# Neighbours' weights in a PSUM bank, key monomials spread over three chunks, and layer 2's first loads ahead of the fall-back loops

## The chip, the cores and the metric

The kernel runs on one core of a Trainium2 chip. The metric is device time in microseconds, from the start to the end of one execution. The kernel before took 4456.89 us (median of 3 runs, 4449.6 to 4462.39). The execution that was profiled took 4452.14 us, and its profile spans 4450.3 us. The mean TensorE clock granted in it was 0.842 of full speed.

Engine names: PE is TensorE (PEld its weight loads), DVE is VectorE, ACT is ScalarE, POOL is GpSimd, and SP issues most of the DMAs. SBUF is the large on-chip memory, PSUM the smaller one into which PE writes, in eight banks. L840 is line 840 of the kernel.

## The reference, cut to what matters

Four graph layers work on 2708 nodes with 128 channels and a dense 2708 x 2708 matrix `adj`, about 0.15% of which (with the diagonal) is not zero. Each layer is x = x + layer(relu(layernorm(x))). The change lies in layer 1 and at the start of layer 2:

```python
# layer 1: attention, 128 heads d of 8 channels, over all nodes
q = (x @ Wq.T).reshape(d, n, h)          # k and v in the same way
a = jnp.einsum('dnh,dmh->dnm', q, k) * scale
a = a + spatial_encoding + edge_encoding # both are adj
a = jax.nn.softmax(a, axis=2)
out = jnp.einsum('dnm,dmh->dnh', a, v)
return out.reshape(n, h * d) @ Wo.T

# layer 2: mean over the graph, two weights, batch norm
deg = adjacency_matrix.sum(axis=1, keepdims=True)
agg = adjacency_matrix.T @ node_features / deg
h = agg @ W_n.T + b_n + node_features @ W_c.T + b_c
# then normalised over the nodes, scaled, relu
```

## The kernel before, in words

The nodes lie in 22 row tiles of up to 128 rows, the last of 20. Layer 0 and the projections to q, k and v come first; layer 1's heads run from about 468 to 3923 us of the span; layers 2 and 3 follow.

**The heads.** Layer 1 never forms the 2708 x 2708 logits. It expands the exponential into monomials of the eight channels of q and of k. For each head d:

- `keys(d)` has GpSimd multiply the key monomials `bk` and `fk` together: twelve multiplications, given out one at a time by the generator `features` (with `mul_g`, whose multiplications are recorded at L1010). `with_values(d, h)` then has GpSimd form `y`, the monomials times the values, for each half h of the row tiles (also L1010).
- `queries(d)` does the same for q on DVE (L1007), reading one operand in PSUM (`q_ps`).
- `moments` has PE sum `fk` times `y` over the nodes in `m_ps` (L1048), and `weighted` has DVE multiply that by constants (L1058).
- For each of six chunks of up to four row tiles (`NCH` is 6), `turn` has PE transpose query monomials into `f_ps` (L1074), which ACT copies to `fT` (L1076); `evaluate` has PE multiply them with the moments into `g_ps` (L1086), and DVE multiply the result by `bq` (`z`, L1094) and sum it (`o_raw`, L1100).

**The neighbours.** Where `adj` isn't zero, a correction is added for each true neighbour. `from_neighbours` does this in 121 blocks, each of one neighbour for each row of a tile. Per block, GpSimd gathers `c_kv` (and once per tile `c_q`) with an indirect DMA; `logits` has DVE multiply keys with queries (`c_z`, L840) and reduce that to `c_c`, one number per row and head (L844); `weigh` has ACT take the exponential in place (L852) and scale it by the edge's weight (L854); `values` of the block before has ACT copy `c_c` into the ninth column (L869), DVE multiply values with `c_c` (L870) into `c_v`, or for a tile's first neighbour straight into `c_acc`, and GpSimd add `c_v` to `c_acc` (L879). A finished tile is stored to `more_n` by an indirect DMA (L887).

**What sets the order.** Everything in the heads is inside `with tc.manual_schedule()`, so each engine takes its instructions in the order in which the program text issues them. Waits between engines are put in from the tiles that they share. In each chunk the loop runs `evaluate`, three steps of `queries`, the next `turn`, a part of `moments`, and then on average `PACE` = 1.45 steps of the generator `first`. This generator runs a search for the neighbours, a re-ordering of q, k and v by node, the sorting of rows, and then `from_neighbours`, which occupies about 1320 to 3322 us. All twelve multiplications of `keys(d + 2)` are issued in one go in chunk 0; `with_values` follows in chunks 2 and 5.

**After the neighbours.** When `first` is done, the list `beside` is worked on, three calls of `step` per chunk. It has 32 times `normalise(g)` (DMAs bring the sums and the corrections of four heads, GpSimd adds them at L930, DVE divides at L932 and L933, SP stores `o_c`) and 22 times `project_out` (SP loads `o_cr`, L499; PE multiplies it with `woT` in four groups of two, L505, each into a buffer of `ps_t`; DVE adds each group to `x_sb`, L508). What remains when the heads end is drained in the loop `while beside or under_way`.

**Between layers 1 and 2.** L1186 to L1223 check from bounds whether the expansion is accurate enough and the neighbour lists long enough. The result, `flag`, is the trip count of three fall-back loops, which in this case run zero times. At a loop's entry each engine waits for all the others and for all DMA queues. Then layer 2 opens its pools, loads and transposes its weights (`wnT`, `wcT`), normalises x (`norm_relu`), spreads the reciprocal degrees over all partitions (`diB`, 22 pairs of a small matmul and an ACT copy), and multiplies `adj`, loaded by row tiles into four buffers (L1339), into `pg` (L1341).

`ps_t`, with two buffers of one bank each, serves `f_ps`, the groups of `project_out` and some transposes. With `m_ps` (1), `g_ps` (2 buffers of two banks) and `q_ps` (1) all eight banks are in use.

Of the kernel before, what the change touches and what calls it, by code (L numbers as in the profile page):

```python
# [9 lines left out]
FP = mybir.dt.float32  # L10
AF = mybir.ActivationFunctionType
# [38 lines left out]
def gnn4_kernel(  # L50
# [75 lines left out]
    few = keep.tile([P, 1], FP, name="few")  # L126

# [388 lines left out]
    with ExitStack() as ph:  # L516
# [8 lines left out]
        ps_t = ph.enter_context(tc.tile_pool(name="l1_pst", bufs=2, space=PSUM))  # L525
        ps_m = ph.enter_context(tc.tile_pool(name="l1_psm", bufs=1, space=PSUM))
        ps_g = ph.enter_context(tc.tile_pool(name="l1_psg", bufs=2, space=PSUM))
        ps_q = ph.enter_context(tc.tile_pool(name="l1_psq", bufs=1, space=PSUM))

# [272 lines left out]
        def from_neighbours():  # L802
# [6 lines left out]
            qs, kvs, cs, accs = {}, {}, {}, {}  # L809
            done = []  # L810
# [23 lines left out]
            def logits(b):  # L834
                t, s0, w = todo[b]
                sz = rows[t][1]
                cs[b] = sm.tile([P, S, C], FP, name="c_c")
                for e in range(w):
                    z = tm.tile([P, C, HEAD], FP, name="c_z", tag="tmp")
                    nc.vector.tensor_tensor(  # L840
                        z[:sz], kvs[b][:sz, e, :, 0], qs[t][:sz], ALU.mult
                    )
                    yield
                    nc.vector.reduce_sum(cs[b][:sz, e], z[:sz], axis=AX.X)  # L844
                    yield
# [169 lines left out]
        def keys(d):  # L1015

            k = got[d // GRP][0][:, d % GRP, :, k_at]
            fks[d] = fp.tile([P, NT, F_ALL], FP, name="fk")
            run(features(mul_g, k, bks[d % 2], fks[d]))
# [86 lines left out]
        with tc.manual_schedule():  # L1106
# [4 lines left out]
            keys(0)  # L1111
# [3 lines left out]
            keys(1)  # L1115
# [10 lines left out]
            for d in range(D):  # L1126
                asked = queries(d + 1) if d + 1 < D else iter(())
                for c in range(NCH):
                    if d + 2 < D and c == 0:
                        while len(got) <= (d + 2) // GRP:  # L1130
                            run(soon.pop(0))
                        keys(d + 2)
# [29 lines left out]
                if (d + 2) % GRP == 0 and (d + 2) // GRP + 1 < NG:  # L1162
                    soon.append(prepare((d + 2) // GRP + 1, got))
            while beside or under_way:
# [4 lines left out]
    with ExitStack() as ph:  # L1169
        gp = ph.enter_context(tc.tile_pool(name="l1g", bufs=1))  # L1170
        gw = ph.enter_context(tc.tile_pool(name="l1g_w", bufs=2))
        g_l = ph.enter_context(tc.tile_pool(name="l1g_l", bufs=1, space=PSUM))
        g_t = ph.enter_context(tc.tile_pool(name="l1g_t", bufs=1, space=PSUM))
        g_o = ph.enter_context(tc.tile_pool(name="l1g_o", bufs=1, space=PSUM))
        q_f = dram.tile([N, P, HEAD], FP, name="q_f")
        k_f = dram.tile([N, P, HEAD], FP, name="k_f")
        v_f = dram.tile([N, P, VW], FP, name="v_f")
        o_f = dram.tile([N, P, HEAD], FP, name="o_f")

        nc.vector.memset(top, 0.0)
        p2 = gp.tile([C, 2], FP, name="p2")
        for e in range(2):
            pt = g_t.tile([P, BK], FP, name="g_tr", tag="tr")  # L1186
            nc.tensor.transpose(pt[:C, :P], most2[:, e], ident)
            nc.vector.tensor_reduce(p2[:, e : e + 1], pt[:C, :P], axis=AX.X, op=ALU.max)
        nc.vector.tensor_tensor(top[:, 0:1], p2[:, 0:1], p2[:, 1:2], ALU.mult)
        nc.vector.tensor_tensor(top[:, 1:2], p2[:, 0:1], p2[:, 1:2], ALU.max)  # L1190
        nc.vector.tensor_reduce(top[:, 2:3], nval, axis=AX.XY, op=ALU.max)
        nc.vector.tensor_reduce(top[:, 3:4], nval, axis=AX.XY, op=ALU.min)
        low = gp.tile([P, 1], FP, name="low")
        nc.vector.tensor_reduce(low, least, axis=AX.X, op=ALU.min)
        nc.vector.tensor_tensor(top[:, 3:4], top[:, 3:4], low, ALU.min)
        nc.vector.tensor_scalar_mul(top[:, 3:4], top[:, 3:4], -1.0)
        nc.vector.tensor_reduce(low, below, axis=AX.X, op=ALU.max)
        nc.vector.tensor_tensor(top[:, 3:4], top[:, 3:4], low, ALU.max)
        nc.vector.tensor_tensor(top[:, 3:4], top[:, 3:4], full, ALU.max)
        pt = g_t.tile([P, BK], FP, name="g_tr", tag="tr")  # L1200
        nc.tensor.transpose(pt[:4, :P], top, ident)
        t4 = gp.tile([4, 1], FP, name="top4")
        nc.vector.tensor_reduce(t4, pt[:4, :P], axis=AX.X, op=ALU.max)
        pt = g_t.tile([P, BK], FP, name="g_tr", tag="tr")
        nc.tensor.transpose(pt[:1, :4], t4, ident[:4, :4])
        bnd = gp.tile([1, 6], FP, name="bound")
        nc.vector.tensor_copy(bnd[:, :4], pt[:1, :4])
        nc.vector.tensor_scalar(
            bnd[:, 4:5], bnd[:, 0:1], MAX_LOGIT**2, None, ALU.is_le
        )  # L1210
        nc.vector.tensor_scalar(bnd[:, 2:3], bnd[:, 2:3], float(MAX_ADJ), None, ALU.is_le)
        nc.vector.tensor_tensor(bnd[:, 4:5], bnd[:, 4:5], bnd[:, 2:3], ALU.mult)
        nc.vector.tensor_scalar(bnd[:, 1:2], bnd[:, 1:2], MOST**2, None, ALU.is_le)
        nc.vector.tensor_tensor(bnd[:, 4:5], bnd[:, 4:5], bnd[:, 1:2], ALU.mult)
        nc.vector.tensor_scalar(bnd[:, 5:6], bnd[:, 3:4], 0.0, None, ALU.is_le)
        nc.vector.tensor_scalar(ovf, bnd[:, 5:6], -1.0, 1.0, ALU.mult, ALU.add)
        pt = g_t.tile([P, BK], FP, name="g_tr", tag="tr")
        nc.tensor.matmul(pt[:, :1], ones[0:1], bnd[:, 5:6], start=True, stop=True)
        nc.vector.tensor_copy(few, pt[:, :1])
        nc.vector.tensor_tensor(bnd[:, 4:5], bnd[:, 4:5], bnd[:, 5:6], ALU.mult)  # L1220
        flag = gp.tile([1, 2], I32, name="flag")
        nc.vector.tensor_scalar(flag[:, 0:1], bnd[:, 4:5], -1.0, 1.0, ALU.mult, ALU.add)
        nc.vector.tensor_scalar(  # L1223
            flag[:, 1:2], bnd[:, 4:5], -float(C), float(C), ALU.mult, ALU.add
        )
        once = nc.values_load(flag[:, 0:1], min_val=0, max_val=1)
        heads = nc.values_load(flag[:, 1:2], min_val=0, max_val=C)

        with tc.For_i(0, once):
            for r0, sz in rows:  # L1230
                for at, dst in ((0, q_f), (HEAD, k_f), (2 * HEAD, v_f)):
                    b = gw.tile([P, P, dst.shape[2]], FP, name="bounce", tag="b")
                    nc.sync.dma_start(
                        b[:, :sz], qkv_c[:, r0 : r0 + sz, at : at + dst.shape[2]]
                    )
                    nc.sync.dma_start(dst[r0 : r0 + sz].rearrange("r c h -> c r h"), b[:, :sz])

        def flat(src):
            return src.rearrange("r c h -> (r c) h")

        with tc.For_i(0, heads) as d:
            nat = []
            for src in (q_f, k_f, v_f):
                a = gp.tile([P, NT, src.shape[2]], FP, name=f"g_nat{len(nat)}")
                f = flat(src)[bass.ds(d * N, N)]
                load_rows(nc.sync, a, f)
                nat.append(a)
            q, k, v = nat
            kT = gp.tile([HEAD, N], FP, name="g_kT")
            for t, (r0, sz) in enumerate(rows):  # L1250
                pt = g_t.tile([P, BK], FP, name="g_tr", tag="tr")
                nc.tensor.transpose(pt[:HEAD, :sz], k[:sz, t], ident[:sz, :sz])
                nc.vector.tensor_copy(kT[:, r0 : r0 + sz], pt[:HEAD, :sz])
            o = gp.tile([P, NT, HEAD], FP, name="g_o")
            for t, (r0, sz) in enumerate(rows):
                an = gw.tile([P, N], FP, name="g_adj")
                nc.sync.dma_start(an[:sz], adj[r0 : r0 + sz])
                pt = g_t.tile([P, BK], FP, name="g_tr", tag="tr")
                nc.tensor.transpose(pt[:HEAD, :sz], q[:sz, t], ident[:sz, :sz])
                qT = gw.tile([HEAD, P], FP, name="g_qT")  # L1260
                nc.vector.tensor_copy(qT[:, :sz], pt[:HEAD, :sz])
                pl = g_l.tile([P, NC, BK], FP, name="g_l")
                for c, (c0, cw) in enumerate(cols):
                    nc.tensor.matmul(
                        pl[:sz, c, :cw], qT[:, :sz], kT[:, c0 : c0 + cw], start=True, stop=True
                    )
                    nc.vector.scalar_tensor_tensor(
                        an[:sz, c0 : c0 + cw],
                        pl[:sz, c, :cw],
                        0.5,  # L1270
                        an[:sz, c0 : c0 + cw],
                        ALU.mult,
                        ALU.add,
                    )
                mx = gw.tile([P, 1], FP, name="g_mx")
# [326 lines left out]
```

## Time and profile before

| what | value |
|---|---|
| median of 3 runs | 4456.89 us |
| profiled execution | 4452.14 us |
| its span | 4450.3 us |
| PE busy over the span | 3230.9 us, 73% |
| DVE busy | 3549.0 us, 80% |
| ACT busy | 1101.9 us, 25% |
| POOL busy | 2789.4 us, 63% |
| c_z (L840), 121 instructions | 419.5 us, mean 3467 ns |
| c_v (L870), 99 instructions | 244.5 us, mean 2470 ns |

How to read it: busy times count what an engine executes, a stall in the middle of an instruction included. The shares are averages over stages with different limits, so they are not yet a statement on what bounds the kernel. An instruction's line may be that of a helper: all GpSimd multiplications of the heads, whatever they form, are recorded at L1010, and are told apart by their tiles. In the answers shown, `out<-in` are the names of the tiles, `xN` the number of instructions, and `<-DVE x` behind an idle time names what ended it.

### The profile page before, as it was taken

What the parts mean: (1) busy time and instruction counts of PE and PEld (TensorE: products, weight loads), DVE (VectorE), ACT (ScalarE), POOL (GpSimd) and SP (SyncE); (2) the same over time, 40 slices, a digit from 0 to 9 for tenths busy, and PEclk for the clock granted to TensorE, in tenths of its full rate; (3) what the DMA queues carried; (4) which work ended last, traced back from release to release, by engine and by line L of the source; (5) the groups of instructions that cost most, each with busy time, mean ns of one, the idle gap of its engine ahead of it and who ended that gap; (6) DMA issues with size and microseconds to landing.
All of it is one profiled execution on the core that took longest, in us unless ns stands there. A gap on an engine that the chain in (4) does not pass through costs nothing. (4 is left out here: it accounts for less than half of the span.)

```text
span 4450.3 us, 49671 instructions
## 1 busy us (share of the span) xinstructions
PE 3230.9 (73%) x17298; PEld 2879.4 (65%) x17298; DVE 3549.0 (80%) x4852; ACT 1101.9 (25%) x2497; POOL 2789.4 (63%) x2384
## 2 busy tenths in 40 slices
PE   7986788888857777776777766767767788949434
PEld 5953677788756666666666656667657787834223
DVE  5988899987849989999988999999977777840322
ACT  4246233333312222222222222222221111210110
POOL 0001766677767887887878777678876666700266
PEclk9988889899978888888888888888888899979565
DMA  4637344367412222222222222222324454035232
GB/s 181 225 143 304 101 108 123 98 140 178 110 54 80 84 79 90 90 91 81 90 90 91 81 76 96 82 94 97 104 70 105 112 113 96 23 103 203 75 86 70
DMA packets 402006, 480.25 MB, mean 108 GB/s; under 512 B 290672, under 2 KB 322098, under 8 KB 376916
## 3 DMA queue, kind: packets, MB, share of 16 engines
q1 hardware_dynamic: 370140, 308.03, 24.1%
q0 software_dynamic: 31600, 168.86, 11.5%
q8 instruction: 144, 2.36, 0.2%
q14 instruction: 122, 1.00, 0.1%
HBM read 363.13 MB, written 113.67 MB: 107 GB/s over the span
## 5 line engine op out<-in xcount | busy, mean ns | idle before, releaser
L1086 PE MATMUL g_ps<-mw,fT 128*128 128x189 f32 x5632 | 1227.8, 366 | 699.1 <-DVE mw L1058 397.8
L1086 PEld LDWEIGHTS g_ps<-mw,fT 128*128 128x128 f32 x5632 | 1043.2, 215 | 781.0 <-issue 521.9
L1010 POOL TENSOR_TENSOR y<-bk,raw 128x2079 f32<-128x2079 f32 x256 | 976.2, 3814 | 516.1 <-PE m_ps L1048 478.3
L1048 PE MATMUL m_ps<-y,fk 128*128 128x189 f32 (+1 forms) x5632 | 1101.7, 340 | 21.3 <-POOL y L1010 21.3
L1048 PEld LDWEIGHTS m_ps<-y,fk 128*128 128x128 f32 (+1 forms) x5632 | 963.5, 203 | 50.5 <-issue 28.7
L1076 ACT COPY fT<-f_ps 128x512 f32<-128x512 f32 (+1 forms) x768 | 422.7, 550 | 1962.1 <-PE f_ps L1074 1960.1
L1094 DVE TENSOR_TENSOR z<-g_ps,bq 128x756 f32<-128x756 f32 (+1 forms) x768 | 669.4, 872 | 202.4 <-PE g_ps L1086 201.7
L1100 DVE TENSOR_REDUCE o_raw<-z 128x36 f32<-128x756 f32 (+1 forms) x768 | 672.5, 876 | 26.3
L1074 PE MATMUL f_ps<-ident,fq 128*128 128x128 f32 x2816 | 490.3, 299 | 38.9 <-DVE fq L1007 36.2
L1010 POOL TENSOR_TENSOR fk<-bk,raw 128x528 f32<-128x528 f32 (+1 forms) x512 | 508.2, 1021 | 0.0
L1074 PEld LDWEIGHTS f_ps<-ident,fq 128*128 128x128 f32 x2816 | 400.5, 157 | 75.7 <-issue 31.5
L840 DVE TENSOR_TENSOR c_z<-c_kv,c_q 128x1024 f32<-128x1024 f32 (+1 forms) x121 | 419.5, 3467 | 10.6 <-DMA c_kv<-kv_n,srt 10.6
L879 POOL TENSOR_TENSOR c_acc<-c_acc,c_v 128x1152 f32<-128x1152 f32 (+1 forms) x99 | 262.1, 2647 | 165.6 <-DVE c_v L870 119.1
L1010 POOL TENSOR_TENSOR fk<-raw,bk 128x352 f32<-128x352 f32 (+1 forms) x512 | 317.7, 649 | 0.0
L1007 DVE TENSOR_TENSOR fq<-bq,q_ps 128x528 f32<-128x528 f32 (+1 forms) x512 | 288.0, 604 | 0.0
L870 DVE TENSOR_TENSOR c_v<-c_kv,c_c 128x1024 f32<-128x1024 f32 (+1 forms) x99 | 244.5, 2470 | 1.3 <-POOL c_acc L879 1.3
L465 POOL MEMSET qkv<- 128x512 f32 x6 | 6.3, 1083 | 374.8 <-PE l_o L350 255.4
L1010 POOL TENSOR_TENSOR bk<-raw 128x88 f32<-128x88 f32 (+1 forms) x512 | 216.7, 454 | 33.4 <-DMA raw<-qkv_c 32.9
L1420 POOL DMA_INDIRECT g<-gate_d,srt x121 | 122.6, 1013 | 107.7 <-issue 107.7
L825 POOL DMA_INDIRECT c_kv<-kv_n,srt x121 | 137.3, 1135 | 60.2 <-DVE c_acc L870 37.5
L1007 DVE TENSOR_TENSOR fq<-q_ps,bq 128x352 f32<-128x352 f32 (+1 forms) x512 | 171.7, 377 | 0.0
L505 PE MATMUL l_o<-woT,o_cr 128*128 128x128 f32 (+1 forms) x352 | 95.8, 421 | 81.2 <-DMA o_cr<-o_c 40.2
(284 smaller groups left out, 3502.7 us busy)
## 6 DMA issues: line engine op xcount, KB each, us to landing
a_nat<-in_adj_dram SPq DMA_DIRECT2D x32, 1354.0 KB
qkv_c<-qkv SPq DMA_DIRECT2D x5, 6400.0 KB
a<-in_adj_dram SPq DMA_DIRECT2D x21, 1354.0 KB
kv_n<-n_kv SPq DMA_DIRECT2D x32, 672.0 KB
an<-in_adj_dram SPq DMA_DIRECT2D x15, 1354.0 KB
o_g<-o_raw SPq DMA_DIRECT2D x32, 396.0 KB
r_raw<-o_g SPq DMA_DIRECT2D x32, 396.0 KB
r_more<-more_n SPq DMA_DIRECT2D x32, 396.0 KB
```

Source lines behind the costliest of these rows:

```text
L825: nc.gpsimd.indirect_dma_start(out=kvs[b][:sz, e].rearrange("p c e k -> p (c e k)"), out_offset=None, in_=kv_n.rearrange("n c k -> n (c k) ...
L840: nc.vector.tensor_tensor(z[:sz], kvs[b][:sz, e, :, 0], qs[t][:sz], ALU.mult)
L870: nc.vector.tensor_tensor(z[:sz, :, :HEAD], kv[:sz, e, :, 1], c[:sz, e, :, None].to_broadcast([sz, C, HEAD]), ALU.mult,)
L879: nc.gpsimd.tensor_tensor(acc[:sz], acc[:sz], z[:sz], ALU.add)
L1007: nc.vector.tensor_tensor(o, x, y, ALU.mult)
L1010: nc.gpsimd.tensor_tensor(o, x, y, ALU.mult)
L1048: nc.tensor.matmul(pms[d][:, : B_ALL * VW], fks[d][:sz, t], ys[d, h][:sz, m].rearrange("p k b -> p (k b)"), start=t == 0, stop=t == NT - 1,)
L1074: nc.tensor.transpose(pt[:, m], fqs[d][:, t0 + m], ident)
L1076: nc.scalar.copy(fts[d, c][:, :n], pt[:, :n])
L1086: nc.tensor.matmul(pg[:, m, : B_ALL * VW], ft[:, m], mws[d].rearrange("p k b -> p (k b)"), start=True, stop=True,)
L1094: nc.vector.tensor_tensor(z[:, :n], pg[:, :n, : B_ALL * VW].rearrange("p t (k b) -> p t k b", k=VW), bqs[d % 2][:, t0 : t0 + n, None, :B_A ...
L1100: nc.vector.reduce_sum(ros[g][:, t0 : t0 + n, i], z[:, :n], axis=AX.X,)
```

## The change

It has three parts.

1. `c_c` is no longer a tile of the SBUF pool `sm` (two buffers) but one half of a single PSUM tile `c_two`, chosen by the block's parity. `c_two` fills one bank, and for that `ps_t` goes from two buffers to one.
2. `keys` becomes a generator. In `keys(d + 2)` five multiplications are issued in chunk 0, five in chunk 1 and the rest in chunk 2, ahead of `with_values`.
3. The bound check moves ahead of the drain, into the heads' pools; `flag` moves to the pool `keep`. Layer 2's pools are opened before the fall-back loops, and `wnT`, `wcT`, the bias columns, `di`, `diB` and the first four loads of `adj` are issued there; the loops' pools lie on top. `norm_relu` and the adjacency product stay behind the loops.

```diff
-        ps_t = ph.enter_context(tc.tile_pool(name="l1_pst", bufs=2, space=PSUM))
+        ps_t = ph.enter_context(tc.tile_pool(name="l1_pst", bufs=1, space=PSUM))
...
+        ps_c = ph.enter_context(tc.tile_pool(name="l1_psc", bufs=1, space=PSUM))
...
+            c_two = ps_c.tile([P, 2, S, C], FP, name="c_c")
...
-                cs[b] = sm.tile([P, S, C], FP, name="c_c")
+                cs[b] = c_two[:, b % 2]
...
-            run(features(mul_g, k, bks[d % 2], fks[d]))
+            yield from features(mul_g, k, bks[d % 2], fks[d])
...
-                        keys(d + 2)
+                        keyed = keys(d + 2)
+                    if d + 2 < D:
+                        for _ in range(5 if c < 2 else NCH * 3):
+                            next(keyed, None)
...
+            nc.vector.memset(top, 0.0)
+            p2 = sm.tile([C, 2], FP, name="p2")
...
+            nc.vector.tensor_scalar(
+                flag[:, 1:2], bnd[:, 4:5], -float(C), float(C), ALU.mult, ALU.add
+            )
+
             while beside or under_way:
                 if not step(n, NG):
                     n += 1
...
+        with tc.tile_pool(name="l2_ps0", bufs=2, space=PSUM) as ps:
+            wnT = transposed(lp, wk_pool, ps, wn2, "wnT")
+            wcT = transposed(lp, wk_pool, ps, wc2, "wcT")
...
+            diB = lp.tile([P, N], FP, name="diB")
+            for t, (r0, sz) in enumerate(rows):
+                dg = lp.tile([P, P], FP, name="dg", tag="dg", bufs=2)
+                nc.vector.tensor_scalar_mul(dg[:sz, :sz], ident[:sz, :sz], di[:sz, t : t + 1])
+                pd = ps.tile([P, BK], FP, name="d_ps", tag="tr")
+                nc.tensor.matmul(pd[:, :sz], ones[:sz], dg[:sz, :sz], start=True, stop=True)
+                nc.scalar.copy(diB[:, r0 : r0 + sz], pd[:, :sz])
+        for t in range(min(4, NT)):
+            rows_of_adj2(t)
+
+
+        with ExitStack() as gh:
...
+            once = nc.values_load(flag[:, 0:1], min_val=0, max_val=1)
+            heads = nc.values_load(flag[:, 1:2], min_val=0, max_val=C)
```

## The prediction

> **What bounds the kernel now.** I read the windows by stage first, because the 80% that DVE is busy over the whole span mixes stages with different limits. Columns: stretch and us, busy us and (x instructions) of PE, PEld, DVE, ACT, POOL, then the PE clock granted, the DMA share and GB/s.
>
> ```profile
> 468.00:1225.00 757.00, 630.34 (x3693) 590.73 (x3693) 678.27 (x997) 260.86 (x502) 522.04 (x477) 0.91 0.49 120
> 1225.00:3322.00 2097.00, 1468.53 (x7914) 1376.68 (x7913) 1917.43 (x2253) 468.84 (x1182) 1652.94 (x1329) 0.83 0.26 85
> 3322.00:3923.00 601.00, 502.00 (x2847) 473.38 (x2845) 457.11 (x739) 111.89 (x259) 402.30 (x334) 0.91 0.37 85
> 3923.00:3969.00 46.00, 16.33 (x69) 13.94 (x69) 10.60 (x44) 0.00 (x0) 4.74 (x3) 0.58 0.38 96
> 3969.00:4000.00 31.00, 9.77 (x33) 5.44 (x33) 15.96 (x79) 7.28 (x24) 0.13 (x1) 0.57 0.49 189
> ```
>
> The second stretch, where the neighbour blocks run beside the heads, is 47% of the span, and DVE is busy 91% of it (94% in 1445 to 3300, which holds 64 heads of 29.0 us). So DVE sets the pace there. The tile answers say of what its time consists (min/median/max ns):
>
> ```profile
> L840 DVE TENSOR_TENSOR c_z<-c_kv,c_q x121: 1215/3453/14609, 1318.7 to 3300.7; 128x1024 f32<-128x1024 f32 x119, 20x1024 f32<-20x1024 f32 x2
> L870 DVE TENSOR_TENSOR c_v<-c_kv,c_c x99: 1212/1653/8760, 1343.7 to 3322.6; 128x1024 f32<-128x1024 f32 x98, 20x1024 f32<-20x1024 f32 x1
> L844 DVE TENSOR_REDUCE c_c<-c_z x121: 1197/1210/1223, 1322.2 to 3305.5; 128x128 f32<-128x1024 f32 x119, 20x128 f32<-20x1024 f32 x2
> ```
>
> The same 1024 elements take 1.2 us or up to 14.6 us in the first two rows, and always 1.2 us in the reduce. The timeline shows what stands beside a long one (start, duration):
>
> ```profile
> 2078.65 10.53 DVE L840 TENSOR_TENSOR c_z<-c_kv,c_q 128x1024 f32<-128x1024 f32 x1
> ...
> 2076.85 1.39 POOL L1010 TENSOR_TENSOR bk<-raw 128x176 f32<-128x176 f32 x4
> 2078.19 2.38 POOL L1010 TENSOR_TENSOR fk<-raw,bk 128x352 f32<-128x352 f32 x4
> 2080.53 3.85 POOL L1010 TENSOR_TENSOR fk<-bk,raw 128x528 f32<-128x528 f32 x4
> 2084.35 3.75 POOL L1010 TENSOR_TENSOR y<-bk,raw 128x2079 f32<-128x2079 f32 x1
> ```
>
> c_z stands until GpSimd's train of twelve key multiplications and one y is over. Summed over its durations, c_z is 419.5 us busy against 121 x 1.22 = 148, so 271 us are standing; c_v and the first-of-tile c_acc are 292.7 against 147, so 146 (125 of them in 1445 to 3300). By the GpSimd operation running meanwhile, I put c_z's standing in 1445 to 3300 at 147 under y, 82 under keys, 32 under the rest, and c_v's at 62 under keys and 58 under y.
>
> **What the Trainium skill says.** "SBUF — State Buffer", section "Who interferes with whom": a DVE instruction that reads two operands from SBUF shares a port pair with GpSimd under an exclusive lock; with one SBUF operand it doesn't. The trace agrees: z, with g_ps in PSUM, averages 0.87 us over both its forms and never stands, while c_v reaches 8.76. "VectorE: DVE Perf Modes", section "The perf-mode tier table": an fp32 tensor_tensor runs at 1x from SBUF and from PSUM, so moving an operand costs no rate. z's 756 elements in 0.93 us and c_v's unhindered 1024 in 1.21 fit that. "PSUM — Partial Sum Buffer", section "PSUM bank collisions raise a hardware error": two engines must not touch one bank at once, so ACT and DVE have to take turns on it. No trace here shows the price.
>
> **The change part by part**, against the profiled execution's 4452.1 us (span 4450.3 and 1.8 around it), which lies 4.8 under the median 4456.9, inside the three runs' 12.8.
>
> *Weights in PSUM.* c_v and c_acc keep one SBUF operand and lose their 146 us of standing. The 1.21 us stay, and so do c_z's, whose operands are both in SBUF. DVE is 94% busy, so I let 0.9 through: -131.
>
> *Keys over three chunks.* The same twelve multiplications, split as 2.3 us (0.48 + 3 x 0.34 + 0.83) in chunk 0, 3.9 in chunk 1 and 1.7 ahead of y in chunk 2, where 7.8 stood together. An operation that comes at random waits in proportion to the sum of squares of the trains: before 7.8², 3.8², 3.8², after 2.3², 3.9², 5.5², 3.8², so 90 becomes 65, or 0.73. That takes 0.27 of c_z's 261: -70. Heads that come faster (29.0 to some 26.5) put the same GpSimd work into less time: +18 on the 191 left. Net -52, of which I count -45, since the trains may still join where GpSimd is behind. Who waits: y of half 0 is now behind only 1.7 us of keys in its chunk, and `moments` needs the keys only a head later. On GpSimd's queue the gathers and c_acc additions of chunks 1 and 2 now stand behind pieces of keys, those of chunk 0 behind less; DVE waits for them 4.2 us today (c_z for c_kv 2.9, c_v for c_acc 1.3), so this is nothing unless gathers come late. In 468 to 1225, PE and DVE bound without blocks, and in the heads of 3322 to 3923 r_on (59.7 us busy against 28.5 unhindered) gains at most 31 x 0.27 = 8, not counted.
>
> *Turns on the bank.* ACT's copy L869 (0.42 us) now comes after the reduce of the next block, and c_v after that copy, all in one bank. Both fall into one chunk in 0.45 of the blocks (1.45 steps a chunk). Two handovers and the copy are about 0.75 us by these rows: 121 x 0.45 x 0.75 = +40. From 0, if other DVE work lies between, to 121 x 0.75 = +91. ACT's exp and scale (0.31 and 0.40) come after c_v and four steps before they are needed: hidden. Behind a waiting ACT stands fT, for which PE's g_ps waits (73.8 us in 1445 to 3300), so part of ACT's waiting may return there; this is in the upper bound.
>
> *One ps_t buffer for two.* For the transposes it is free: `evaluate` of a chunk already waits for the fT copy that empties the buffer before PE comes to the next `turn`. project_out is not free. With two buffers its first two groups ran in one go, and DVE's additions came later together:
>
> ```profile
> 3600.59 2.02 PE L505 MATMUL l_o<-woT,o_cr 128*128 128x128 f32 x8
> 3604.91 0.67 DVE L508 TENSOR_TENSOR x_sb<-x_sb,l_o 128x128 f32<-128x128 f32 x2
> 3605.25 1.22 PE L505 MATMUL l_o<-woT,o_cr 128*128 128x128 f32 x4 [2.64 <-DVE x_sb L508]
> 3606.50 0.29 DVE L508 TENSOR_TENSOR x_sb<-x_sb,l_o 128x128 f32<-128x128 f32 x1 [0.92 <-PE l_o L505]
> ```
>
> PE's third group already waited 2.64 us. With one buffer each further group in a chunk stands for DVE's addition, and the chunk's turn and `evaluate` with it: some 1.9 us per project (two handovers, at the 0.92 and 0.29 just shown plus a start), 18 projects in the loop: +35, from 10 to 60. In the drain after it the additions follow each other in 0.96 us; eight groups become about 0.6 longer: +5.
>
> *Checks and layer 2 earlier.* The bound check ran from 3964.48 to 3968.74 with nothing beside it; now it stands in the 6.4 us in which PE waited for o_cr: -4.3. diB (22 multiplications and copies) leaves the adjacency product, about 6 us of PE there, but DVE and ACT need the time before: -6 if beside the loads, else +8. The four adjacency loads are 1.354 MB each; they landed at 3989.0 to 3998.4, 19.5 us after SP's first layer-2 load at 3978.87. Now they are issued ahead of the loops, and every engine waits at a loop's entry for all queues. Their buffers lie where the drain's tmp tiles lay, so they start only after the last l_o. On SP nothing else is queued behind them but later layer-2 work. What lay after the empty loops (9.7 us) then lies before them: what is saved behind is paid ahead. norm_relu, which the loads used to cover, then stands alone for part of its 16 us. From -12 to +20; I take +8 with diB in it.
>
> Sum: -131 - 45 + 40 + 35 + 5 - 4 + 8 = -92. Span 4358, and by the median of the runs **4365 us**.
>
> **The rivals.** *GpSimd's standing moves on to c_z (gain of 13 to 40).* After a c_v that no longer stands, c_z meets the train that c_v met before. For it: y causes 147 of c_z's 261 and is unchanged, and GpSimd's own 23.1 us per head is not far under 29. Against: c_v's freedom alone takes 2 us of each head. If half of the 131 comes back, the keys give 20 and the turns cost half: -65 - 20 + 20 + 35 + 5 - 4 + 8 = -21, time 4436.
>
> *Broken trains give more (gain of 150 to 260).* If keys never join y, 0.27 becomes 0.5, and turns hide behind other DVE work: -146 - 112 + 10 + 20 + 5 - 4 + 8 = -219, time 4238. The limit is GpSimd's 23.1 us and c_z's own 2.1 per head, about 25.2, so at most 64 x 3.8 = 243 there.
>
> *Slower: c_v waits for ACT.* ACT works in order and waits 961 us in 1445 to 3300 for f_ps. If L869 stands behind an fT whose transposes PE has not begun, the reduce, the copy and c_v become one chain through PE, and DVE, in order, stands with it. The other terms sum to -132, so it decides at 132/121 = 1.1 us per block; at 1.7 instead of 0.33 it is +206 - 132 = +74: 4531. For it: z waits only 42.7 us for PE today, so PE is little behind. That also speaks against it: PE has finished the turn by the time DVE is at the reduce.
>
> *The change does nothing where it counts.* If both contenders were not ports but memory as a whole, c_v would stand as before. z and the reduce, never long, exclude nearly all of that.
>
> **How the numbers follow.** Forecast (-150 to -40) 0.50; more 0.20; gain of 13 to 40 0.14; within 0.3% (13 us, about what a measurement of this kernel tells from no change) 0.08; slower 0.08. So faster 0.84, same 0.08, slower 0.08. The range leaves out slower, half of same and the far third of the larger gain: 4252 to 4450. The likeliest case alone is 4307 to 4417.
>
> **What would show it.** c_v and c_acc at 1.21 to 1.3 us whatever GpSimd does; c_z's mean from 3.47 to 2.5 to 2.9; heads beside neighbours 26.5 to 27.5 us, DVE still over 90% busy. DVE waits for ACT copy L869 near 40 us in all. PE waits l_o for x_sb above today's 29.4 (in 3330 to 3764), by 20 to 40. No stretch of bound checks before the loops, but adjacency loads ahead of them. I am wrong if DVE's share falls below 85% with heads near 29 us (then a new wait has replaced the standing), if c_z's mean rises, or if the gap from the last l_o to the first pg matmul, 36 us now, passes 56.

## The result, and the profile after

The changed kernel took 4410.15 us (median of 4 runs, 4385.7 to 4422.99) against 4459.64 of the kernel before: ratio 0.9894, 95% interval 0.9853 to 0.9935. A second set of runs gave 4384.33 against 4444.4: 0.9844, 0.9805 to 0.9884. Together that is some 1.3%, about 58 us faster. I had said 92. The direction and the range held; the forecast gain was more than half again as large as what came.

The profiled execution took 4385.7 us (span 4383.9), 66 less than the profiled one of before. Single executions of one kernel lie up to 1.3% apart here. Four of the profiles below are of kernels whose code is the same in the 64 heads that lie wholly beside the neighbours (the changed kernel twice, and the two with `project_out` in one group), and these heads took 1771, 1790, 1777 and 1814 us. A difference between two profiles within that spread is read only together with the timed runs.

The windows of the changed kernel, by the same stages as before (columns as in the prediction):

```profile
465.70:1220.00 754.30, 625.25 (x3701) 584.58 (x3702) 679.26 (x996) 261.49 (x503) 522.84 (x478) 0.93 0.50 121
1220.00:3229.00 2009.00, 1446.03 (x7907) 1354.68 (x7906) 1758.65 (x2250) 452.29 (x1183) 1617.46 (x1330) 0.85 0.27 89
3229.00:3848.00 619.00, 520.56 (x2846) 484.75 (x2844) 438.29 (x741) 111.83 (x258) 402.21 (x334) 0.89 0.36 82
3848.00:3900.00 52.00, 23.03 (x75) 16.08 (x74) 14.32 (x53) 0.27 (x1) 5.20 (x4) 0.52 0.37 88
```

Everything that was won lies in the second stretch: 2097 us became 2009. DVE's busy time there fell by 159 us and its idle time rose by 71 (179.6 to 250.4). The stretch after it became 18 us longer, the drain 6.

The tile answers of the changed kernel say what of DVE's time went:

```profile
L843 DVE TENSOR_TENSOR c_z<-c_kv,c_q x121: 1214/2468/12565, 1305.2 to 3212.7; 128x1024 f32<-128x1024 f32 x119, 20x1024 f32<-20x1024 f32 x2
L873 DVE TENSOR_TENSOR c_v<-c_kv,c_c x99: 1202/1216/1233, 1343.8 to 3229.9; 128x1024 f32<-128x1024 f32 x98, 20x1024 f32<-20x1024 f32 x1
```

c_v, which took up to 8.76 us, takes 1.23 at most. c_z's busy time over the span fell only from 419.5 to 404.1 us, and in a second profile of the changed kernel it was 421.2; its median is lower, its sum hardly.

DVE's waits, in the 64 heads from the 41st to the 105th weighted moments (1854.1 us before, 1771.0 after), first of the kernel before, then of the changed one (total us, times, longest):

```profile
DVE c_acc L870 <- DMA more_n<-c_acc,srt: 47.5, 11, 12.2
```

```profile
DVE c_acc L873 <- ACT c_acc L872: 102.5, 19, 10.9
DVE c_v L873 <- ACT c_v L872: 14.3, 29, 0.5
```

The turn on the bank (c_v behind ACT's copy) is 14.3 us, half a microsecond at a time; DVE's wait for PE hardly changed (42.7 and 45.2 us). The large new wait is that of a tile's first block. One instance on the timeline of the changed kernel (start, duration):

```profile
2067.77 3.79 POOL L1013 TENSOR_TENSOR y<-bk,raw 128x2079 f32<-128x2079 f32 x1
2071.73 1.02 POOL L890 DMA_INDIRECT more_n<-c_acc,srt  x1 [0.17 <-POOL y L1013]
...
2075.75 1.22 DVE L873 TENSOR_TENSOR c_acc<-c_kv,c_c 128x1024 f32<-128x1024 f32 x1 [4.20 <-ACT c_acc L872]
...
2075.33 0.39 ACT L872 COPY c_acc<-c_c 128x128 f32<-128x128 f32 x1 [7.33 <-DMA more_n<-c_acc,srt]
```

GpSimd finishes a y before it issues the store of the finished tile at 2071.73; the store lands some 3.6 us after that; only then may ACT write the ninth column of the single c_acc buffer, and DVE follows. DVE is named as waiting for ACT, but ACT waited for the store.

Last, the drain of the changed kernel, where every group waits for the addition before it:

```profile
3886.11 0.29 DVE L509 TENSOR_TENSOR x_sb<-x_sb,l_o 128x128 f32<-128x128 f32 x1 [5.01 <-PE l_o L506]
...
3886.45 1.32 PE L506 MATMUL l_o<-woT,o_cr 128*128 128x128 f32 x4 [0.38 <-DVE x_sb L509]
3887.81 0.29 DVE L509 TENSOR_TENSOR x_sb<-x_sb,l_o 128x128 f32<-128x128 f32 x1 [1.42 <-PE l_o L506]
```

The additions come 1.70 us apart, where they came 0.96 apart.

### The profile page after: what moved, and what is told of

It is laid out like the page before. It is cut to its first block, busy times and chain, and to the rows that moved or that the text cites. A ratio compares the mean times of both kernels' runs of the same rounds, so it can differ in the third digit from the quotient of the medians.

```text
span 4383.9 us, 49356 instructions
## 1 busy us (share of the span) xinstructions
PE 3231.9 (74%) x17298; PEld 2865.9 (65%) x17298; DVE 3374.6 (77%) x4852; ACT 1086.1 (25%) x2497; POOL 2755.9 (63%) x2384
## 5 line engine op out<-in xcount | busy, mean ns | idle before, releaser
L1089 PE MATMUL g_ps<-mw,fT 128*128 128x189 f32 x5632 | 1208.6, 361 | 586.2 <-DVE mw L1061 250.4
L1089 PEld LDWEIGHTS g_ps<-mw,fT 128*128 128x128 f32 x5632 | 1030.1, 212 | 666.2 <-ACT fT L1079 287.1
L1051 PEld LDWEIGHTS m_ps<-y,fk 128*128 128x128 f32 (+1 forms) x5632 | 962.3, 203 | 49.6 <-issue 28.9
L1013 POOL TENSOR_TENSOR fk<-bk,raw 128x528 f32<-128x528 f32 (+1 forms) x512 | 497.5, 999 | 0.5
L843 DVE TENSOR_TENSOR c_z<-c_kv,c_q 128x1024 f32<-128x1024 f32 (+1 forms) x121 | 404.1, 3339 | 14.5 <-DMA c_kv<-kv_n,srt 14.5
L1013 POOL TENSOR_TENSOR bk<-raw 128x88 f32<-128x88 f32 (+1 forms) x512 | 205.2, 433 | 33.6 <-DMA raw<-qkv_c 33.1
L506 PE MATMUL l_o<-woT,o_cr 128*128 128x128 f32 (+1 forms) x352 | 108.3, 446 | 77.9 <-DVE x_sb L509 47.7
L506 PEld LDWEIGHTS l_o<-woT,o_cr 128*128 128x128 f32 (+1 forms) x352 | 88.3, 321 | 95.9 <-DVE x_sb L509 60.4
```

What stands on the lines that cost most here:

```text
L506: nc.tensor.matmul(po[:sz], o[:, :sz, k], woT[:, k], start=k == k0, stop=k == k0 + kw - 1)
L843: nc.vector.tensor_tensor(z[:sz], kvs[b][:sz, e, :, 0], qs[t][:sz], ALU.mult)
L1013: nc.gpsimd.tensor_tensor(o, x, y, ALU.mult)
L1051: nc.tensor.matmul(pms[d][:, : B_ALL * VW], fks[d][:sz, t], ys[d, h][:sz, m].rearrange("p k b -> p (k b)"), start=t == 0, stop=t == NT - 1,)
L1089: nc.tensor.matmul(pg[:, m, : B_ALL * VW], ft[:, m], mws[d].rearrange("p k b -> p (k b)"), start=True, stop=True,)
```

## The experiments

All ratios are against the kernel before, run on the same chip in the same set.

### The parts, each alone

Four kernels: the bank with its one ps_t buffer, the spread keys, the moved checks and loads, and one ps_t buffer with c_c still in SBUF.

```diff
# bank_alone
-        ps_t = ph.enter_context(tc.tile_pool(name="l1_pst", bufs=2, space=PSUM))
+        ps_t = ph.enter_context(tc.tile_pool(name="l1_pst", bufs=1, space=PSUM))
+        ps_c = ph.enter_context(tc.tile_pool(name="l1_psc", bufs=1, space=PSUM))
-                cs[b] = sm.tile([P, S, C], FP, name="c_c")
+                cs[b] = c_two[:, b % 2]
# one_buffer_alone
-        ps_t = ph.enter_context(tc.tile_pool(name="l1_pst", bufs=2, space=PSUM))
+        ps_t = ph.enter_context(tc.tile_pool(name="l1_pst", bufs=1, space=PSUM))
# keys_alone: the edit to keys() and its calls
# layer2_alone: the third part of the change
```

> Only the weights in the PSUM bank (and with it one ps_t buffer). Theory 1 (the gain is c_v's freedom from GpSimd, less the turns on the bank): c_v and c_acc at 1.22 us always, c_z's standing stays near 260 to 270 us, DVE waits for ACT's copy into c_acc near 100 us where it waited 57 for the store; in all 35 to 60 us faster than before. Theory 2 (the spread keys carry the gain, the bank only trades standing for waiting): within 15 us of before. Theory 3 (freed time returns as standing of c_z): c_z's standing grows by 50 us or more, gain under 25.

> Only the key monomials spread over three chunks. Theory 1 (trains become shorter): c_z's standing from 271 to 200 us, c_v's from 145 to 110, 40 to 70 us faster. Theory 2 (GpSimd is behind with its queue, so that the pieces join other work: the changed kernel's mean train was 6.2 us, not shorter than 5.5): standing of both within 10% of before, time within 15 us.

> Only the bound check and layer 2's first loads moved. Theory 1: the loads are paid ahead of the loops and norm_relu stands alone behind them: 5 to 12 us slower than before, all of it between the last head and the adjacency product. Theory 2 (the loads are hidden in the drain): 4 to 10 us faster.

> Only ps_t with one buffer, c_c stays in SBUF. Theory 1: heads before and beside the neighbours unchanged within 5 us, each project_out some 1 us longer, drain some 5 us longer: 15 to 25 us slower. Theory 2 (one buffer costs nothing, since the order already implies the waits): within 5 us.

| kernel | ratio | 95% interval |
|---|---|---|
| bank with one buffer | 0.9936 | 0.9915 to 0.9957 |
| spread keys | 0.9941 | 0.9923 to 0.9959 |
| checks and layer 2 | 0.9997 | 0.9976 to 1.0017 |
| one buffer, no bank | 1.0163 | 1.0128 to 1.0199 |

The first three sum to -1.26%, which lies between the two figures of the changed kernel (-1.06 and -1.56%): within the noise the parts add up. The surprise is the last row. One buffer costs 1.6%, some 72 us, where both theories allowed 25 at most. The bank itself is then worth 0.9936/1.0163 = 0.978, about 99 us, give or take 18 (93 by the medians of all runs of the two kernels).

With the bank alone, c_v is free of GpSimd:

```profile
L872 DVE TENSOR_TENSOR c_v<-c_kv,c_c x99: 1197/1214/1224, 1354.9 to 3280.8; 128x1024 f32<-128x1024 f32 x98, 20x1024 f32<-20x1024 f32 x1
```

With the keys alone both rows keep their standing (the time by which an operation exceeds its unhindered 1.22 us), yet the kernel is 26 us faster:

```profile
L840 DVE TENSOR_TENSOR c_z<-c_kv,c_q x121: 1215/2973/14635, 1312.2 to 3276.5; 128x1024 f32<-128x1024 f32 x119, 20x1024 f32<-20x1024 f32 x2
L870 DVE TENSOR_TENSOR c_v<-c_kv,c_c x99: 1214/1717/8760, 1340.7 to 3294.1; 128x1024 f32<-128x1024 f32 x98, 20x1024 f32<-20x1024 f32 x1
```

In the 64 heads c_z, c_v and the first products c_acc together stood 381 us there, 386 before. The heads took 1825.8 us instead of 1854.1 (1859.8 with the checks and layer 2 alone, where they have the code of before), and of these 28 us DVE's busy time gave 5. The rest is DVE's wait for the store of a tile, 26.7 us where it was 47.5:

```profile
DVE c_acc L870 <- DMA more_n<-c_acc,srt: 26.7, 11, 6.8
```

From the end of a tile's last c_v to the start of the next tile's c_acc, the chain is GpSimd's last addition, the store's issue and its landing. Over the 21 tiles it took 16.9 us on average before and 15.5 with spread keys: the addition started 0.76 us after c_v instead of 1.56, and the store was issued 9.4 us after the addition's start instead of 10.1. 21 times 1.4 is 29 us. This fits the gain, but it is one profile of each kernel; the last pair of experiments tests it.

One buffer alone: the exchange between PE and DVE from the 106th to the 121st moments, of the kernel before, and then with one buffer.

```profile
PE l_o L505 <- DVE x_sb L508: 29.4, 10, 8.4
DVE x_sb L508 <- PE l_o L505: 28.2, 30, 2.2
```

```profile
DVE x_sb L508 <- PE l_o L505: 59.5, 47, 2.0
...
PE l_o L505 <- DVE x_sb L508: 43.2, 32, 10.4
```

Over its whole span PE also waits where it didn't wait before: a transpose for the sum of the values in `prepare`, which uses the same buffer.

```profile
PE f_ps L1074 <- DVE v_sum L686: 71.2, 26, 6.2
```

In the profiled execution the heads after the neighbours took 630.8 us instead of 605.1, from the last head's product to the last x_sb 50.0 instead of 43.8, and the first 40 heads 6.8 more. The two profiles differ by 45 us in all. That of one buffer is the fastest of its seven executions, 4497.17 us against a median of 4515.6, so that some 27 of the 72 us are in no profile.

In the 64 heads beside the neighbours the sum hardly changed (1858.7 us against 1854.1), but its parts did: c_z, c_v and c_acc stood 338 us instead of 386, and DVE waited longer for the store of a tile, 85.0 us instead of 47.5:

```profile
DVE c_acc L870 <- DMA more_n<-c_acc,srt: 85.0, 15, 12.2
```

No port was touched here. In this pair of profiles, then, the store's wait rises where the standing falls.

### The changed kernel again, and three of its terms taken away

```diff
# after_two_acc
-            qn = lp.tile([P, NT, GRP, HEAD], FP, name="n_q")
+            qn = lp.tile([P, NT, GRP, HEAD], FP, name="n_q", tag="n_q")
-                    accs[t] = lp.tile([P, C, VW], FP, name="c_acc", tag="n_kv")
+                    accs[t] = lp.tile([P, C, VW], FP, name="c_acc", tag=("n_kv", "n_q")[t % 2])
# after_split
-                cs[b] = c_two[:, b % 2]
+                cs[b] = sm.tile([P, S, C], FP, name="c_e")
-                        c[:sz, e], c[:sz, e], AF.Copy, scale=cw[:sz, t, s0 + e : s0 + e + 1]
+                        c_two[:sz, b % 2, e], c[:sz, e], AF.Copy,
+                        scale=cw[:sz, t, s0 + e : s0 + e + 1],
-                    nc.scalar.copy(z[:sz, :, HEAD], c[:sz, e])
+                    nc.scalar.activation(z[:sz, :, HEAD], c[:sz, e], AF.Copy,
+                        scale=cw[:sz, t, s0 + e : s0 + e + 1])
-                        c[:sz, e, :, None].to_broadcast([sz, C, HEAD]),
+                        c_two[:sz, b % 2, e, :, None].to_broadcast([sz, C, HEAD]),
# after_group8
-        for k0, kw in _cuts(HEAD, 2):
+        for k0, kw in _cuts(HEAD, HEAD):
```

> The changed kernel once more, for a narrower interval beside its variants. The parts alone gave 0.9936 (bank), 0.9941 (keys) and 0.9997 (layer 2); if they add up, 0.987 to 0.989. If spread keys and the bank overlap in what they save: 0.990 to 0.994.

> The changed kernel with two buffers for c_acc, taken by turns, so that a tile's first block waits for the store of the tile before the last. Theory 1 (DVE's 102 us of waiting for ACT's copy into c_acc are the store's latency, come up from under the standing that went): that wait under 15 us, heads beside neighbours from 27.7 to 26.3 us, 50 to 90 us faster than the changed kernel. Theory 2 (it is ACT's turn on the bank that makes DVE wait): the wait stays over 60 us, time within 15 us of the changed kernel.

> The changed kernel with the reduce, the exponential and ACT's copy into the ninth column in SBUF; only the scaled weights that c_v reads go to the bank, written by ACT's scaling. The same number of instructions. Theory 1 (turns on the bank cost little, the store's latency much): 0 to 20 us faster than the changed kernel, ACT no longer waits 340 us for the reduce. Theory 2 (turns on the bank are what ate the gain): 40 to 80 us faster.

> The changed kernel with each project_out in one group of eight matmuls and one addition, so that no group waits for the addition before it. Theory 1 (the one ps_t buffer costs 25 us beside the normalisations and 5 to 8 in the drain, by these waits): heads after the neighbours back to 605 us or less from 618, 15 to 30 us faster than the changed kernel. Theory 2 (the buffer costs through the transposes): within 8 us.

| kernel | median us | ratio | 95% interval |
|---|---|---|---|
| changed kernel | 4384.33 | 0.9844 | 0.9805 to 0.9884 |
| two c_acc buffers | 4333.10 | 0.9734 | 0.9700 to 0.9768 |
| split weights | 4343.67 | 0.9777 | 0.9748 to 0.9806 |
| one group of eight | 4381.08 | 0.9836 | 0.9793 to 0.9880 |

Two buffers for c_acc take the wait away and 51 us with it. Their 64 heads, and DVE's wait in them:

```profile
1444.50:3176.40 1731.90, 1280.41 (x7106) 1201.21 (x7104) 1645.02 (x2032) 408.46 (x1071) 1443.13 (x1156) 0.86 0.28 94
```

```profile
DVE c_acc L873 <- ACT c_acc L872: 2.8, 6, 0.5
```

So it was the store, not ACT's turn. Of some 100 us of waiting in either profile of the changed kernel, 39 and 58 were won in these heads; c_z's standing in them was 222 and 242 us there (226 and 270 in the other two profiles with the same heads) and 285 with two buffers.

The split won 41 us by the medians, 30 by the ratios, more than the 0 to 20 that my theory gave it. Its profiled execution, 4388.4 us, was the slowest of its six, so that its stages don't say where. In the group of eight, nothing was won: GpSimd now waited for the loads of normalise (8.9 us in the changed kernel), since fewer steps lay between a load and its use.

```profile
POOL r_raw L933 <- DMA r_more<-more_n: 49.5, 9, 17.8
```

### The combinations

```diff
# after_group8_paced: one group of eight, and in project_out after the addition
-            yield
+            for _ in range(HEAD // 2):
+                yield
# after_split_two: the split and two c_acc buffers
# after_best: these two and the paced group of eight
# before_two_acc: two c_acc buffers in the kernel before
```

> The changed kernel with project_out in one group of eight matmuls and one addition, but with as many steps per project as before, so that normalise is not drawn ahead of its loads (there GpSimd waited 49 us for them when the steps were left out). Theory 1 (the buffer's cost beside the normalisations is the exchange between PE and DVE): heads 104 to 120 from 473 to 450 to 460 us, 12 to 25 us faster than the changed kernel. Theory 2 (it is the transposes): within 8 us.

> The changed kernel with both the split of the weights (only the scaled ones in the bank) and two c_acc buffers. Two buffers alone gave 0.9734 against before, the split alone 0.9777, the changed kernel 0.9844. Theory 1 (turns on the bank hold DVE 14 us and delay ACT's fT, nothing else): 0 to 15 us faster than with two buffers alone. Theory 2 (turns have a cost of 30 to 40 us of their own): 0.963 to 0.967.

> All three: the split of the weights, two c_acc buffers, and project_out in one group with its steps kept. If the three add up: 0.960 to 0.965 against before; if the freed time returns as c_z's standing: not below 0.970.

> The kernel before with two c_acc buffers. Theory 1 (the wait for the store was partly hidden under the standing, and comes up when the standing goes): the 47 us of DVE's wait for it go, a part returns as standing, 10 to 40 us faster than before, less than the 51 that the same edit gave in the changed kernel. Theory 2 (the store's wait is independent of the ports): the same 45 to 55 us.

| kernel | median us | ratio | 95% interval |
|---|---|---|---|
| paced group of eight | 4352.34 | 0.9735 | 0.9698 to 0.9772 |
| split, two c_acc | 4308.11 | 0.9649 | 0.9618 to 0.9680 |
| all three | 4267.22 | 0.9545 | 0.9510 to 0.9580 |
| before with two c_acc | 4418.33 | 0.9900 | 0.9868 to 0.9933 |

With its steps kept, the group of eight is worth some 1% (0.9735, where the changed kernel stood at 0.9844 and 0.9894 in other sets), since it takes away both the exchange and three of four additions. The stretch from the 105th to the 121st head took 437.7 us, 472.8 in the changed kernel, and DVE's wait for PE in it is below that of two buffers and four groups (28.2):

```profile
POOL r_raw L934 <- DMA r_more<-more_n: 26.7, 9, 6.1
...
DVE x_sb L509 <- PE l_o L506: 23.3, 11, 4.3
```

This speaks for the exchange, as predicted, as the buffer's cost beside the normalisations, though the edit takes additions away too. Against the transposes speak the waits of the one-buffer kernel in that stretch: PE waits 2.0 us there for the copy of `v_sum` before a transpose, beside the 59.5 and 43.2 us of the exchange. All three edits together came to 0.9545, a larger gain than the 0.960 to 0.965 of a plain sum.

The split on top of two buffers brings 0.9734 to 0.9649, about 38 us, with some 20 to either side, from two different sets. With the 30 to 41 us of the split alone this says that the turns cost more than the 14 us that DVE waits for them. What they did besides is seen at PE, in the 64 heads, with two c_acc buffers alone and then with the split:

```profile
PE g_ps L1089 <- ACT fT L1079: 130.7, 39, 16.2
```

```profile
PE g_ps L1095 <- ACT fT L1085: 6.0, 8, 1.0
```

ACT, waiting for the reduce of the next block (402.9 us there), held back the fT copies behind it. But that this wait costs time is not shown: DVE's own wait for PE did not fall (47.7 us, then 58.6), and the heads became only 12 us shorter in the profiles, 1731.9 to 1719.9. The profiled execution of the split was the slowest of its six, 35 us above their median. Where the 38 us lie stays open.

In the kernel before, two c_acc buffers win 44 us and the 47.5 us of waiting go; standing does not take them back (382 us against 386). That lies between theory 1 and theory 2, and the interval (30 to 59 us) holds both; what it shows is that the store's wait cost nearly as much before the change as after it.

### Do the spread keys work by the standing?

```diff
-                        keyed = keys(d + 2)
-                    if d + 2 < D:
-                        for _ in range(5 if c < 2 else NCH * 3):
-                            next(keyed, None)
+                        keys(d + 2)
```

> The changed kernel with two c_acc buffers, and with the twelve key multiplications in one go in chunk 0 again. Two buffers with spread keys gave 0.9734. Theory 1 (spread keys saved time by letting GpSimd's addition and store of a finished tile come 1.4 us sooner, 21 times, and not by shorter standing): without the store's wait the spread has nothing left beside the neighbours, and only the 10 to 15 us in the heads after them go: 0.974 to 0.978. Theory 2 (shorter trains shorten c_z's standing once c_v is out of the way): 0.981 to 0.985.

> The fastest kernel so far (split weights, two c_acc buffers, project_out in one group; 0.9545) with the key multiplications in one go again. Theory 1: 0.955 to 0.959. Theory 2: 0.961 or more.

With the keys in one go again, the changed kernel with two c_acc buffers ran at 0.9673 (0.9634 to 0.9712; spread 0.9734), and the kernel with all three edits at 0.9500 (0.9456 to 0.9544; spread 0.9545). Neither lost anything, which contradicts theory 2 and goes beyond theory 1. That keys in one go are faster is not shown by these runs: the spread kernels ran in other sets, and the ratio of the changed kernel alone differed by 0.5% between two sets. The 64 heads and c_z, with two buffers and keys in one go:

```profile
1436.60:3124.20 1687.60, 1269.65 (x7106) 1191.08 (x7104) 1586.73 (x2032) 409.47 (x1071) 1455.26 (x1156) 0.87 0.29 97
```

```profile
L843 DVE TENSOR_TENSOR c_z<-c_kv,c_q x121: 1214/2922/11722, 1321.4 to 3125.9; 128x1024 f32<-128x1024 f32 x119, 20x1024 f32<-20x1024 f32 x2
```

1687.6 us against 1731.9, and c_z stood 226 us against 285; in the pair with all three edits 230 against 265. One such pair says little, since the four profiles with the same heads ran from 222 to 270. But the three with spread keys and two buffers stand at 265 to 285 (280 in the split), the two in one go at 226 and 230. The spread keys win only in the heads after the neighbours (473.6 against 483.3 us from the 105th to the 121st, 435.6 against 446.5 in the other pair).

4233.08 us, the median of the last kernel (4215.24 to 4263.45), is 5.0% under the kernel before and some 3.7% under the changed one: weights in PSUM, with only the scaled ones in the bank, two c_acc buffers, project_out in one group, keys in one go.

## Why the prediction was right and wrong

The parts sum to 54 us of gain instead of 92. Two terms of the forecast failed. The one ps_t buffer cost 72 us instead of 40: its mechanism was seen, its size was wrong. The spread keys gave 26 us instead of 45, and not by the mechanism stated. The other two terms missed by 8 and 5 us the other way.

| step | predicted us | by timed runs |
|---|---|---|
| weights in PSUM, turns included | -131 + 40 = -91 | 0.978: -99 |
| one ps_t buffer, drain included | +35 + 5 = +40 | 1.0163: +72 |
| keys over three chunks | -45 | 0.9941: -26 |
| checks and layer 2 | -4 + 8 = +4 | 0.9997: -1 |
| sum | -92 | -54; changed kernel -47 and -69 |

**What bounds the kernel, and the ports: right.** c_v came to 1.21 us whatever GpSimd did, in every kernel with the weights in PSUM. DVE stayed the bound of the neighbours' heads. The section of the Trainium skill's "SBUF — State Buffer" that I drew on ("Who interferes with whom") is borne out: one operand moved, and 123 us of standing in 64 heads went to nothing.

**Turns on the bank: a sum that fits by luck, from other terms.** I priced two handovers in 0.45 of the blocks, 40 us. DVE's wait for ACT's copies into c_v is 14, half a microsecond for each c_v behind ACT's copy. That is DVE's share in the price of the turns that the Trainium skill asks for ("PSUM — Partial Sum Buffer", section "PSUM bank collisions raise a hardware error"); ACT, behind the reduce, waits 338.5 us. What grew more among DVE's waits is that for the store of a finished tile, 47.5 us before and 102.5 after. The prediction went through what DVE waits for on GpSimd's queue and left out this one, the largest. That a DVE that stands less comes sooner to the store fits the one-buffer kernel as well, but no run isolates it. The heads took 27.7 us (26.5 to 27.5 forecast; 27.7 to 28.3 in the four profiles with these heads) with DVE 89% busy (over 90 forecast). The delay of fT behind a waiting ACT, which I put into the upper bound, is seen at PE; whether it is part of the split's 38 us stays open.

**Keys over three chunks: the step that failed in its mechanism.** "An operation that comes at random waits in proportion to the sum of squares of the trains" did not hold here. The trains were miscounted from the start: the prediction squares keys and y apart, while in the timeline that it shows y follows the keys without a gap and c_z stands over both. When spread, the pieces still join each other, additions, gathers and y (with keys alone the longest c_z again took 14.6 us beside a y, a sum and all twelve multiplications in a row). GpSimd's mean train was 5.5 us before, 5.4 with keys alone, 6.2 in the changed kernel. The sum of squares over twice the time, which is the mean wait of an operation that comes at random, did fall with keys alone, from 3.83 to 3.35 us, but c_z's standing did not (261 and 265 us). Nor was the formula's size right: c_z stood 2.4 us on average before, less than 3.83. It doesn't come at random, since its place among GpSimd's pieces is set by the order, and a train doesn't always hold it to the end (last section). With two c_acc buffers the sum of squares gives 3.86 us spread and 4.52 in one go, so less standing when spread, and 285 us stood against 226. c_z's mean, forecast at 2.5 to 2.9 us, was 3.34. Why c_z stood more with two buffers and spread keys, beyond that it then met keys for 113 us instead of 74 and y for 127 instead of 99, I can't say. What the 26 us came from instead is, by the profiles, additions and stores that no longer queued behind twelve multiplications, and some 12 us in the heads after the neighbours (453.7 us from the 105th to the 121st, 465.3 before). That nothing was lost by joining the keys again once the store's wait was gone agrees with this.

**One ps_t buffer: the mechanism right, the size off, and one sentence wrong.** The exchange beside the normalisations was seen as described, though more on DVE's side: PE's wait rose by 14 us in the one-buffer kernel (20 to 40 forecast), DVE's by 31. The drain rose by 7.5 us in the changed kernel (43.8 to 51.3) for a predicted 5. But the whole came to 72 instead of 40, the largest error in the sum. "For the transposes it is free" holds between chunks and not where `prepare` puts its sum of values into the same buffer: 71.2 us of PE waiting, 26 times, of which about 5 us show in the heads before the neighbours (721 us, then 726). Some 27 us of the 72 are in no profile, and their cause stays open.

**Checks and layer 2: right within the noise.** The stretch from the last x_sb to the first adjacency product, and the product, of the kernel before and then of the changed one:

```profile
3964.40:3993.00 28.60, 3.92 (x16) 2.44 (x17) 13.62 (x88) 4.04 (x12) 0.13 (x1) 0.57 0.34 123
3993.00:4102.10 109.10, 109.09 (x323) 54.52 (x322) 11.34 (x38) 8.56 (x35) 0.00 (x0) 0.98 0.66 240
```

```profile
3897.20:3930.10 32.90, 16.02 (x54) 12.11 (x55) 16.23 (x86) 9.76 (x34) 0.00 (x0) 0.50 0.47 173
3930.10:4032.90 102.80, 102.80 (x279) 49.08 (x278) 6.33 (x18) 3.28 (x13) 0.00 (x0) 0.99 0.64 232
```

4.3 us longer ahead, 6.3 shorter in the product, as the loads and diB were said to move: paid ahead, saved behind. One reading of the prediction was off: the gap from the last l_o to the first pg matmul was 28.9 us before, not 36, and became 33.3.

**The rivals.** "GpSimd's standing moves on to c_z" is not seen between the kernel before and the changed one (261 us; 222 and 242). But it is not excluded: in the kernel with one buffer alone, from which the bank starts, c_z stood 191 us, the profiles of the changed kernel's heads lie at 222 to 270, and it was 285 when the store's wait went while the keys were spread. "Broken trains give more" fell: GpSimd's work in the 64 heads lay in 269 trains before, in 273 with keys alone and in 233 in the changed kernel. "c_v waits for ACT" happened in small, 14.3 us over the 112 blocks of the 64 heads or 0.13 per block, far under the 1.1 from which it would have decided. "The change does nothing where it counts" is excluded by c_v's row.

## What to carry to other kernels

Before a stall on the bounding engine is priced, list that engine's other waits as well: here the largest was for a single buffer that was written again only 17 us after its last product, and whose second copy was worth 44 us before the change and 51 after it. A freed PSUM bank has a price to be worked out for every user of the pool that gave it up, helpers included. Before spreading an engine's work to shorten another engine's stalls, look whether it has gaps to spread it into: here the queue was behind, the pieces joined, and what changed was the order.

## What was not expected of the hardware

A DVE operation that reads two SBUF operands can be held over many GpSimd instructions in a row: the longest c_z of before, 14.6 us, lay beside a y, a sum and twelve key multiplications one behind the other, of which none took longer than 3.78. But it is not always held to the end. Of the 76 c_z of more than 2 us in that profile, 21 got in between two instructions that followed each other without a gap, and then GpSimd's took about 1 us longer:

```profile
1384.48 5.42 DVE L840 TENSOR_TENSOR c_z<-c_kv,c_q 128x1024 f32<-128x1024 f32 x1
1384.95 3.79 POOL L1010 TENSOR_TENSOR y<-bk,raw 128x2079 f32<-128x2079 f32 x1
1388.68 2.48 POOL L1010 TENSOR_TENSOR bk<-raw 128x176 f32<-128x176 f32 x4
```

The same four multiplications took 1.39 us at 2076.85, with no c_z beside them. What decides between the two is not shown. The contention cost both engines: with c_v free, GpSimd's busy time in the 64 heads fell as well, from 1476 to 1446 us. With one operand in PSUM, 99 of 99 c_v took 1.20 to 1.23 us in the changed kernel.
